# Single PSUM banks for the feed-forward's inner units, and an empty step between a norm's variance and the use of its root

## The chip, the cores and the metric

The kernel is one program on one core of a Trainium2 chip. It runs two transformer blocks over a batch of 2 sequences of 2048 tokens, 128 channels wide, in float32. The metric is the time on the device in microseconds; the median of several runs is given. The engines are named as in the profile: PE is TensorE (matrix products and transposes), PEld its weight loads, ACT is ScalarE, DVE is VectorE, POOL is GpSimd, SP is SyncE (it issues most DMA transfers). PSUM is the memory that PE writes to, SBUF the one that the other operands lie in.

## The reference, cut to what matters

Each of the two blocks is an attention layer and then a stack of local-attention layers with feed-forward; both are modulated by a conditioning vector. The first block has a chunked attention with a memory and then 6 local layers (16 heads, window 32); the second has a causal linear attention with its own norms and a feed-forward, and then 2 local layers (8 heads, window 64). A local layer is, cut short:

```python
h = shift(x)                        # half of the channels come from the token before
q, k, v = split(h @ Wqkv)           # q and k: l2norm, scale, rotary tables
x = x + local_attention(q, k, v) @ Wo
...
mu = h.mean(-1); var = ((h - mu) ** 2).mean(-1)
xn = (h - mu) / sqrt(var + 1e-5) * g + b
a, gate = split(xn @ W1 + b1)       # 341 inner units each
x = x + (a * gelu(gate)) @ W2 + b2
```

The linear attention between the two stacks has three norms of the same form: one ahead of q, k and v, one ahead of its feed-forward, and one that makes the input of the second stack.

## The kernel before, in words

The profile's first 640 us or so are the first block's attention (`l0_attention`), which the change does not touch. Everything else is in `local_models`. It treats 8 local layers (6 of the first model, 2 of the second) as one long list of tiles: 32 tiles of 128 tokens per layer (16 places in the sequence for each of the 2 sequences, the sequences alternating). Channels or head columns lie on the partitions in the layer's state, tokens on the partitions during attention.

A single loop over the tiles (L1505 and on) works on several of them at once. In turn i it writes down:

- the scores of tile i+1 (`ps_s`), their exponential on ACT (`weights_exp`, L1008) and their norm;
- the projection of q and k of tile i+3 (`project`: `ps_qk` L871, the square `sq` on ACT L873, rotary products `r` and `t` on DVE, sums on POOL). A tile of the first model has two projections, one of the second model has one;
- **place A** for a feed-forward step, between the first and the second projection;
- the transposes of tile i's weights (`ps_pT` L1026, copied by ACT, L1027), the values of tile i+2 (`ps_v` L951, copied by ACT, L952), the weighted sum of tile i (`ps_o` L1043), the transposes of q and k of tile i+2 (`ps_turn` L923), the transposes of the sum (`ps_oT` L1059, copied by ACT L1060);
- **place B** for a feed-forward step;
- the output projection of tile i (`ps_y` L1071).

After four tiles of one sequence a feed-forward over their 512 tokens is appended to the list `steps` as six small functions: `centre` (one matmul that subtracts the mean, and a square on ACT, L1098), `variance` (four matmuls to `ps_var` L1107, plus epsilon on DVE `fve` L1112, power -1/2 on POOL `frt` L1114), `scale` (four transposes that spread the root, `ps_r` L1120, product on DVE `fx` L1123), `gate` (three matmuls `ps_f` L1141, of 128, 128 and 85 units, and three Gelus on ACT L1151), `up` (the other three `ps_f`, and a product with the Gelus on DVE L1158) and `down` (`ps_fy` L1166, and the sum into the state on DVE, L1172). `step()` runs the first of the list. So a tile takes up to two steps; two feed-forwards fall due in every eight tiles, which have sixteen places.

The linear attention is cut in the same way into 27 steps per block of 512 tokens (`linear`, L1236), some of them an empty `rest`. Its list, `lsteps`, has six places a tile and is filled after the last layer of the first model; its eight blocks run among the last tiles of that model and the first of the second. A tile of the second model's first layer that needs a block not yet finished runs `lstep` until it is (the loop on `ready`). The steps of its norms use the same `centre`, `variance` and `scaled`.

PSUM has two pools: `psA` with two slots of two banks (`wide`: `ps_qk`, `ps_s`, two of the three parts of `ps_f`, and three tiles of the linear attention), and `psT` with four slots of one bank (`bank`: everything else named above, and the third part of `ps_f`). A slot is taken in turn when its earlier tile has been read.

The order in which the instructions stand on each engine is not that of the code alone: a list scheduler sets it when the program is built, with the order of the code as priority and its own estimates of duration. It can bring an instruction forward past others on its engine.

Of the kernel before, what the change touches and what calls it, by code (L numbers as in the profile page):

```python
# [24 lines left out]
HSZ = (128, 128, 85)  # L25
# [47 lines left out]
def tile_kernel(ctx: ExitStack, tc: tile.TileContext, a: dict, out: bass.AP):  # L73
# [27 lines left out]
    def bc(ap, shape):  # L101
        return ap.to_broadcast(list(shape))
# [605 lines left out]
    def local_models(mA, mB, hs0):  # L708
# [3 lines left out]
        wk = ctx2.enter_context(tc.tile_pool(name="f_k", bufs=1))  # L712
        lw = ctx2.enter_context(tc.tile_pool(name="l_w", bufs=1))
# [3 lines left out]
        def wide(name):  # L717

            return psA.tile([128, 1024], F32, tag="A", name=f"ps_{name}")

        def bank(name):
            return psT.tile([128, 512], F32, tag="T", name=f"ps_{name}")
# [362 lines left out]
        def step():  # L1085
            if steps:
                steps.pop(0)()

        def lstep():
            if lsteps:  # L1090
                lsteps.pop(0)()


        def centre(S, x, pool, keep):
            p = bank("c")
            nc.tensor.matmul(p, lhsT=cen, rhs=x, start=True, stop=True)  # L1096
            S["sq"] = pool.tile([128, 512], F32, name="fsq")
            nc.scalar.activation(S["sq"], p, AF.Square)  # L1098
            if keep:
                S["xc"] = pool.tile([128, 512], F32, tag="t1", name="xc")  # L1100
                nc.scalar.copy(S["xc"], p)

        def variance(S, pool):
            p = bank("var")
            sq = S.pop("sq")
            for j in range(4):
                nc.tensor.matmul(  # L1107
                    p[:, j:j + 1], lhsT=sq[:, j * 128:(j + 1) * 128], rhs=onesm[:, 0:1],
                    start=True, stop=True,
                )  # L1110
            ve = pool.tile([128, 4], F32, name="fve")
            nc.vector.tensor_scalar(ve, p[:, 0:4], 1e-5, None, ALU.add)  # L1112
            S["rt"] = pool.tile([128, 4], F32, name="frt")
            nc.gpsimd.tensor_tensor(S["rt"], ve, bc(nhalf, (128, 4)), ALU.pow)  # L1114

        def scaled(S, x, out):
            p = bank("r")
            rt = S.pop("rt")
            for j in range(4):
                nc.tensor.transpose(  # L1120
                    p[:, j * 128:(j + 1) * 128], bc(rt[:, j:j + 1], (128, 128)), ident
                )
            nc.vector.tensor_tensor(out, x, p, ALU.mult)  # L1123


        def feed_forward(g, b, blk):
            m, l = layers[g]
            n0 = blk * 512
            x = hs[1][:, b, n0:n0 + 512]
            S = {}  # L1130

            def scale():
                S["x"] = wk.tile([128, 512], F32, tag="fsq", name="fx")
                scaled(S, x, S["x"])

            def hidden(base):
                pw = wide("f")
                ps_ = [pw[:, 0:512], pw[:, 512:1024], bank("f")]
                for c, sz in enumerate(HSZ):
                    o = base + 128 * c  # L1140
                    nc.tensor.matmul(  # L1141
                        ps_[c][0:sz], lhsT=wts[g, "w1"][:, o:o + sz], rhs=S["x"],
                        start=True, stop=True,
                    )
                return ps_

            def gate():
                for c, p in enumerate(hidden(HID)):
                    sz = HSZ[c]
                    u = S[c] = wk.tile([128, 512], F32, name=f"u{c}")  # L1150
                    nc.scalar.activation(  # L1151
                        u[0:sz], p[0:sz], AF.Gelu, bias=wts[g, "c"][0:sz, 3 + c:4 + c]
                    )

            def up():
                for c, p in enumerate(hidden(0)):
                    sz = HSZ[c]
                    nc.vector.scalar_tensor_tensor(  # L1158
                        S[c][0:sz], p[0:sz], wts[g, "c"][0:sz, c:c + 1], S[c][0:sz],
                        ALU.add, ALU.mult,  # L1160
                    )

            def down():
                p = bank("fy")
                for c, sz in enumerate(HSZ):
                    nc.tensor.matmul(  # L1166
                        p, lhsT=wts[g, "w2"][0:sz, c, :], rhs=S[c][0:sz],
                        start=(c == 0), stop=(c == 2),
                    )
                for lo, sh in ((0, 0), (64, 1)):  # L1170
                    cs = slice(n0 + sh, n0 + sh + 512)
                    nc.vector.scalar_tensor_tensor(  # L1172
                        hs[0][lo:lo + 64, b, cs], p[lo:lo + 64, :], m.vec[lo:lo + 64, l, 8:9],
                        hs[1][lo:lo + 64, b, cs], ALU.add, ALU.add,
                    )
                if l == m.depth - 1:
                    lsteps.extend((linear if m is models[0] else output)(b, blk))

            steps.extend((
                lambda: centre(S, x, wk, False), lambda: variance(S, wk), scale, gate, up, down,  # L1180
            ))

        def outer(b, k, gate, x):
# [55 lines left out]
        def linear(b, k):  # L1239
            S = {}  # L1240
# [8 lines left out]
            def a0():  # L1249
                outer(b, k, mA, S["x"])  # L1250

            def rest():
                pass

            def a3():
                xc = S.pop("xc")
# [140 lines left out]
            def f3():  # L1397
# [9 lines left out]
                ready.add((b, k))  # L1407

            return (
                fetch, rest, a0, lambda: centre(S, S["x"], lw, True), lambda: variance(S, lw), a3,  # L1410
                rest, lambda: centre(S, S["h"], lw, False), b2, b3, b4, rest, c1, c2, c3, c4, d1,
                rest, lambda: centre(S, S["x1"], lw, False), lambda: variance(S, lw), d4, e1, e2,
                rest, lambda: centre(S, S.pop("x"), lw, True), lambda: variance(S, lw), f3,
            )


# [37 lines left out]
        for i in range(-3, n):  # L1454
            j = i + 3
            lstep()
            if 0 <= i + 1 < n:
                scores(i + 1)
# [3 lines left out]
            if j < n:  # L1462
                g, b, t = tiles[j]
                jj = j % per
                nu = len(layers[g][0].units)
                more = g < last
                if g == second and t % 4 == 0:
                    while (b, t // 4) not in ready:
                        lstep()
                project(j, 0)  # L1470
                if more and jj == 4:
                    load_proj(g + 1, 0)
                if more and jj == 6 and g + 1 == second:
                    models[1].consts()
                if jj == 6 and g == second - 1:
                    linear_consts()
                if more and jj == 8:
                    factors(g + 1)
                    if 2 == 2:
                        load_out(g + 1)  # L1480
                if more and jj == 18:
                    load_ff(g + 1)
                if more and jj == 22:
                    fold_ff(g + 1)
                if more and jj == per - 1:
                    load_proj(g + 1, 1)
                lstep()
# [23 lines left out]
            if i >= 0:  # L1511
                g, b, t = tiles[i]
                project_out(i)
                if 2 == 1 and i % per == per - 1 and g < last:
                    load_out(g + 1)
                if t % 4 == 3:
                    feed_forward(g, b, t // 4)
# [9 lines left out]
    with ExitStack() as ctx2:  # L1527
        local_models(m0, m1, hs0)
# [63 lines left out]
```

## Time and profile before

| what | value |
|---|---|
| median of 3 runs | 5047.73 us (5043.81 to 5053.04) |
| the profiled execution's own time | 5053.27 us |
| its span | 5051.4 us |
| mean granted clock of PE | 0.959 |
| instructions | 171478 |
| `ps_f` matmuls (L1141) | 768, 600 ns each, 365.5 us busy |
| Gelu of the feed-forward, 128 partitions (L1151) | 128, 683 ns each |
| table loads of ACT at L1151, L1008, L1381 | 62, 68 and 7 of 1283 ns |
| root on POOL (`frt` L1114) | 96, 1026 ns each |
| `ps_r` transposes (L1120) | 352, 286 ns each; 23.5 us idle before them |

In the tables of waits, a line names the engine, the tile and line of the instruction that waited, what released it, and then the microseconds in total, the number of waits and the longest. In the timeline, a line is start, duration, engine, line, operation, the tile written and the tiles read, and a count where several alike are put together; in square brackets is the idle time ahead of it. A table load (`ACT_TABLE_LOAD`) is what ACT does when the next function is not among those loaded: here between Exp and Gelu.

### The profile page before, as it was taken

The page shows a single profiled execution, that of the slowest core. Times are in us where ns is not written, and L with a number is a line of the kernel's source. Part 1 is how long each engine was busy: PE and PEld are TensorE (multiplying, and loading weights), DVE is VectorE, ACT ScalarE, POOL GpSimd, SP SyncE. Part 2 cuts the span into 40 slices and gives each one's busy share as a digit, 9 for nine tenths or more (in the row PEclk, how much of TensorE's full clock was granted, in tenths as well). Part 3 has the DMA queues.
Part 4 walks back from the last instruction along what each step waited for, and adds up shares of the span by engine and source line. Part 5 has one row for each costly group of instructions (what it writes and reads, how often), then busy time and mean ns, then how long its engine had stood idle before and what let it go on. Part 6 is the DMA issues. An engine that isn't in the chain of part 4 may idle for free.

```text
span 5051.4 us, 171478 instructions
## 1 busy us (share of the span) xinstructions
PE 4682.5 (93%) x75042; PEld 3190.3 (63%) x75042; DVE 3883.5 (77%) x6760; ACT 2796.3 (55%) x4645; POOL 2761.1 (55%) x1650
## 2 busy tenths in 40 slices
PE   5667799999999999999999999999999998999998
PEld 4445566666666666666666666666666665566565
DVE  6993488788887887788887788787767766688886
ACT  3323356666666665566665566566555654555554
POOL 3331366666665666566666666665544533355553
PEclk8777799999999999999999999999999999999999
DMA  2000222222222322232222322232222211111111
GB/s 76 1 1 24 83 69 66 63 71 74 70 63 63 82 70 63 62 81 72 63 64 65 81 67 64 64 82 64 52 53 54 54 44 36 41 46 48 53 54 40
DMA packets 222491, 295.63 MB, mean 59 GB/s; under 512 B 75657, under 2 KB 95409, under 8 KB 221745
## 3 DMA queue, kind: packets, MB, share of 16 engines
q1 hardware_dynamic: 221744, 284.67, 21.8%
q8 instruction: 592, 9.70, 0.8%
q14 instruction: 155, 1.26, 0.1%
HBM read 40.98 MB, written 10.75 MB: 10 GB/s over the span
## 4 chain that ended last, share of the span: by engine, by line
PE 75%; DVE 6%; ACT 4%; issue 2%; POOL 2%; DMA 0%; SPq 0%; ACTq 0%; POOLq 0%; DVEq 0%
PE ps_qk L871 15%; PE ps_y L1071 8%; PE ps_turn L923 8%; PE ps_o L1043 7%; PE ps_s L991 7%; PE ps_v L951 6%; PE ps_f L1141 6%; PE ps_oT L1059 4%; PE ps_pT L1026 4%; PE ps_fy L1166 3%; PE ps_var L1107 1%; PE ps_c L1096 1%; PE ps_s L982 1%; POOL r L892 1%; ACT sq L873 1%
## 5 line engine op out<-in xcount | busy, mean ns | idle before, releaser
L892 POOL TENSOR_TENSOR r<-r,t 128x1024 f32<-128x1024 f32 x448 | 1059.9, 2366 | 1162.4 <-DVE t L886 1075.2
L873 ACT ACTIVATE sq<-ps_qk 128x1024 f32<-128x1024 f32 x448 | 459.1, 1025 | 1369.4 <-PE ps_qk L871 1353.2
L904 POOL TENSOR_TENSOR r<-r,rq_y 128x1024 f32<-128x1024 f32 x448 | 845.5, 1905 | 268.0 <-DVE rq_y L180 267.1
L871 PE MATMUL ps_qk<-wp,hs 128*128 128x512 f32 x1792 | 883.6, 616 | 30.1 <-DVE rq_y L180 15.4
L886 DVE TENSOR_TENSOR t<-ps_qk,tb 128x1024 f32<-128x1024 f32 (+1 forms) x512 | 552.8, 1080 | 180.5 <-POOL r L892 180.4
L1017 POOL TENSOR_TENSOR sm<-sm,rs 128x1024 f32<-128x1024 f32 x256 | 488.0, 1906 | 293.6 <-DVE rs L1016 196.2
L881 DVE TENSOR_TENSOR r<-ps_qk,tb 128x1024 f32<-128x1024 f32 (+1 forms) x512 | 547.7, 1070 | 103.1 <-ACT sq L873 102.1
L897 DVE TENSOR_REDUCE ps_qk<-sq 128x16 f32<-128x1024 f32 x448 | 549.6, 1227 | 13.5
L871 PEld LDWEIGHTS ps_qk<-wp,hs 128*128 128x128 f32 x1792 | 311.6, 191 | 351.5 <-issue 260.2
L1071 PEld LDWEIGHTS ps_y<-oT,wo 128*128 128x128 f32 x3584 | 440.8, 193 | 122.4 <-issue 71.1
L1071 PE MATMUL ps_y<-oT,wo 128*128 128x128 f32 x3584 | 482.8, 282 | 18.7 <-ACT oT L1060 18.2
L923 PE MATMUL ps_turn<-ident,r 128*128 128x128 f32 x3584 | 470.6, 281 | 22.9 <-issue 12.0
L1043 PEld LDWEIGHTS ps_o<-v,pT 64*32 64x32 f32 (+1 forms) x26624 | 343.6, 108 | 226.9 <-ACT pT L1027 114.9
L951 PE MATMUL ps_v<-wp,hs 128*128 128x512 f32 x896 | 446.9, 598 | 5.9 <-ACT o L1436 3.7
L999 DVE TENSOR_REDUCE mx<-ps_s 128x16 f32<-128x1024 f32 (+1 forms) x256 | 312.9, 1222 | 166.4 <-PE ps_s L991 162.1
L1043 PE MATMUL ps_o<-v,pT 64*32 64x64 f32 (+1 forms) x26624 | 392.5, 222 | 41.0 <-ACT pT L1027 23.3
L923 PEld LDWEIGHTS ps_turn<-ident,r 128*128 128x128 f32 x3584 | 395.2, 143 | 54.4 <-issue 15.8
L991 PE MATMUL ps_s<-kT,qT 64*32 64x64 f32 (+1 forms) x26624 | 400.5, 230 | 3.9 <-ACT kT L928 3.2
L1049 ACT COPY on<-ps_o 128x512 f32<-128x512 f32 x448 | 244.4, 589 | 244.1 <-PE ps_o L1043 244.1
L991 PEld LDWEIGHTS ps_s<-kT,qT 64*32 64x32 f32 (+1 forms) x26624 | 330.1, 107 | 70.3 <-issue 37.3
L1141 PE MATMUL ps_f<-fx,w 128*128 128x512 f32 (+1 forms) x768 | 365.5, 600 | 2.6 <-DVE fx L1123 1.7
L1026 PEld LDWEIGHTS ps_pT<-ident,sm 128*128 128x128 f32 x2048 | 245.7, 142 | 149.6 <-issue 142.1
(266 smaller groups left out, 7693.6 us busy)
## 6 DMA issues: line engine op xcount, KB each, us to landing
v<-vn SPq DMA_DIRECT2D x1276, 128.0 KB
v<-vn SPq DMA_DIRECT2D x744, 64.0 KB
v<-vn SPq DMA_DIRECT2D x64, 256.0 KB
wp<-in_L_ffn_Wqkv SPq DMA_DIRECT2D x20, 512.0 KB
xD<-xb SPq DMA_DIRECT2D x24, 256.0 KB
xb<-xD SPq DMA_DIRECT2D x24, 256.0 KB
cs<-in_cos SPq DMA_DIRECT2D x128, 32.0 KB
cs<-in_sin SPq DMA_DIRECT2D x128, 32.0 KB
```

Source lines behind the costliest of these rows:

```text
L871: nc.tensor.matmul(pq[:, js], lhsT=hw, rhs=wts[g, u][:, js], start=True, stop=True)
L881: nc.vector.tensor_tensor(r[:, es].rearrange("p (h d) -> p h d", d=DH), pq[:, es].rearrange("p (h d) -> p h d", d=DH), bc(tb[:, 0, s].unsq ...
L886: nc.vector.tensor_tensor(t2[:, es].rearrange("p (h s d) -> p h s d", s=2, d=32), pq[:, es].rearrange("p (h s d) -> p h s d", s=2, d=32)[: ...
L892: nc.gpsimd.tensor_tensor(r, r, t2, ALU.add)
L897: nc.vector.tensor_reduce(pq[:, 16 * v:16 * v + 16], st[i].pop(("sq", v)).rearrange("p (h d) -> p h d", d=DH), AX.X, ALU.add,)
L904: nc.gpsimd.tensor_tensor(rv, rv, bc(y[:, 16 * v:16 * v + 16].unsqueeze(2), (128, 16, DH)), ALU.mult)
L923: nc.tensor.transpose(p[:, c * 128:(c + 1) * 128], r[:, cs], ident)
L951: nc.tensor.matmul(p, lhsT=hw, rhs=wv, start=True, stop=True)
L991: nc.tensor.matmul(sp[W * w:W * w + W, c0:c0 + 2 * W], lhsT=qT[64 * q:64 * q + 64, cc, W * w:W * w + W], rhs=kT[64 * q:64 * q + 64, cc, W ...
L1043: nc.tensor.matmul(po[s][W * w:W * w + W, co:co + 64], lhsT=pT[kp, q, c, W * w:W * w + W], rhs=v2[kp, w, co:co + 64], start=True, stop=True,)
L1071: nc.tensor.matmul(py[:, 0:128], lhsT=wts[g, "o"][:, c * NO + s, :], rhs=oT[:, s, c, :], start=(c + s == 0), stop=(c == 3 and s == NO - 1),)
L1141: nc.tensor.matmul(ps_[c][0:sz], lhsT=wts[g, "w1"][:, o:o + sz], rhs=S["x"], start=True, stop=True,)
```

## The change

Three edits, all in `local_models`:

1. `hidden`, which both `gate` and `up` call, takes three single banks for its three parts instead of one wide slot and a bank. The feed-forward no longer uses `psA`.
2. `rest`, an empty function, stands outside `linear` so that both lists can use it, and the feed-forward's list has it between `variance` and `scale`: seven steps instead of six.
3. The linear attention's list has it in three places more, between `variance` and the step that uses the root (`a3`, `d4`, `f3`): 30 steps instead of 27. The norm in `b2` and `b3` is as it was.

No instruction is added, removed or altered by it, apart from what the scheduler reorders and from the table loads that follow from ACT's order.

```diff
+        def rest():
+            pass
+
         def lstep():
...
             def hidden(base):
-                pw = wide("f")
-                ps_ = [pw[:, 0:512], pw[:, 512:1024], bank("f")]
+                ps_ = [bank("f") for _ in HSZ]
                 for c, sz in enumerate(HSZ):
...
             steps.extend((
-                lambda: centre(S, x, wk, False), lambda: variance(S, wk), scale, gate, up, down,
+                lambda: centre(S, x, wk, False), lambda: variance(S, wk), rest, scale, gate, up,
+                down,
             ))
...
-            def rest():
-                pass
...
             return (
-                fetch, rest, a0, lambda: centre(S, S["x"], lw, True), lambda: variance(S, lw), a3,
+                fetch, rest, a0, lambda: centre(S, S["x"], lw, True), lambda: variance(S, lw), rest,
+                a3,
                 rest, lambda: centre(S, S["h"], lw, False), b2, b3, b4, rest, c1, c2, c3, c4, d1,
-                rest, lambda: centre(S, S["x1"], lw, False), lambda: variance(S, lw), d4, e1, e2,
-                rest, lambda: centre(S, S.pop("x"), lw, True), lambda: variance(S, lw), f3,
+                rest, lambda: centre(S, S["x1"], lw, False), lambda: variance(S, lw), rest,
+                d4, e1, e2,
+                rest, lambda: centre(S, S.pop("x"), lw, True), lambda: variance(S, lw), rest,
+                f3,
             )
```

## The prediction

> **What bounds the kernel now.** I read the page first (busy shares, slices, chain), then busy time by stage, TensorE's waits by stage, then the timeline of single tiles.
>
> ```profile
> span 5051.4 us, 171478 instructions
> ...
> PE 4682.5 (93%) x75042; PEld 3190.3 (63%) x75042; DVE 3883.5 (77%) x6760; ACT 2796.3 (55%) x4645; POOL 2761.1 (55%) x1650
> ...
> PE 75%; DVE 6%; ACT 4%; issue 2%; POOL 2%; DMA 0%; SPq 0%; ACTq 0%; POOLq 0%; DVEq 0%
> ```
>
> TensorE is busy 93% of the span and makes 75% of the chain; no other engine makes more than 6%. Cut by stage (us, then busy us and counts of PE, PEld, DVE, ACT, POOL, clock, DMA share, GB/s):
>
> ```profile
> 0.00:820.00 820.00, 615.46 (x8421) 433.14 (x8422) 575.60 (x994) 316.05 (x607) 320.24 (x199) 0.82 0.16 44
> 820.00:4080.00 3260.00, 3177.12 (x58858) 2186.42 (x58857) 2588.08 (x4250) 1961.45 (x3213) 1993.21 (x1164) 0.99 0.26 67
> 4080.00:5051.00 971.00, 889.96 (x7765) 570.78 (x7764) 719.82 (x1517) 518.83 (x827) 447.64 (x288) 0.97 0.16 44
> ```
>
> Between 820 and 4080 us TensorE is idle for 82.9 us of 3260, after that for 81 us of 971. A change that alters no matmul can win only from these 164 us. What they wait for, in the two windows:
>
> ```profile
> PE ps_o L1043 <- issue: 17.4, 10, 2.6
> PE ps_y L1071 <- ACT oT L1060: 14.4, 38, 0.7
> PE ps_turn L923 <- issue: 12.0, 12, 2.4
> PE ps_qk L871 <- DVE rq_y L180: 11.2, 5, 2.7
> PE ps_r L1120 <- POOL frt L1114: 8.7, 6, 2.3
> ```
> ```profile
> PE ps_o L1043 <- ACT pT L1027: 21.3, 33, 2.8
> PE ps_r L1120 <- POOL frt L1114: 14.7, 8, 3.6
> ```
>
> (us, times, longest.) The wait that the empty places address, frt before ps_r, sums to 23.5 us in 14 cases. Each lies at 3605 us or later, most of them up to 4400 us, where the linear attention's norms run among the tiles; in the six steady layers of the first model there is none. A wide PSUM slot held by the feed-forward shows nowhere as such a wait. The last view is the tile whose first feed-forward place holds `up`, in the third layer:
>
> ```profile
> 2023.21 1.28 ACT L1151 ACT_TABLE_LOAD   x1
> ...
> 2027.70 1.98 PE L871 MATMUL ps_qk<-wp,hs 128*128 128x512 f32 x4
> ...
> 2029.72 1.02 ACT L873 ACTIVATE sq<-ps_qk 128x1024 f32<-128x1024 f32 x1 [3.38 <-PE ps_qk L871]
> ...
> 2030.77 1.28 ACT L1008 ACT_TABLE_LOAD   x1
> ...
> 2036.56 1.57 PE L1043 MATMUL ps_o<-v,pT 64*32 64x64 f32 x128
> ```
>
> ScalarE was idle for 3.38 us ahead of sq, so a Gelu and its table load late in a tile are paid from slack. Between the projections and ps_o it has little: sq, exp, sq, two pT copies must all be done before ps_o.
>
> **What the Trainium skill says.** "ScalarE: Activation LUTs", Table sets: the hidden batching unit, puts exp and gelu in different sets and says to batch by set; What ACT_TABLE_LOAD costs prices a switch at some 2.7 us with its drain. The trace agrees that they switch: 138 loads at 1.283 us each; I use 1.28. "PSUM — Partial Sum Buffer", Specifications, has 8 banks of 2 KiB per partition, and its rule on one matmul's output limits that to a bank. So the kernel's two wide slots and four single ones are all there is: what the feed-forward frees in one pool it takes from the other. No page bears on the scheduling of the steps.
>
> **The change part by part.** Times are from T0, the end of a tile's first ps_qk; durations are those of the steady tiles in before's timeline and its groups (three Gelus 1.83, a pair of pT copies 1.07, exp 1.05), and the order on each engine is that of the changed program as built.
>
> 1. The empty places issue no instruction and no DMA, but move all later steps. There are two feed-forward places a tile, A between the two projections and B ahead of ps_y, and two feed-forwards per eight tiles. Before, six steps each: A holds centre, scale, up; B holds variance, gate, down. With seven, the first one's gate and the second one's variance, scale and up fall in A, the first one's up and the second's centre and gate in B. One gate in two now stands in A.
>
> 2. Norms of the steady layers: TensorE's work between ps_var and ps_r grows from 5.0 to 13.6 us, but no wait stood there. Gain 0. The rq_y waits (five of about 2.3 us, one per layer, behind POOL's tables) keep their cause; 0.
>
> 3. Gate in A, first model (six layers of four such tiles: 24). ScalarE's order becomes sq, exp, load, three Gelus, sq, two pT copies: 1.03+1.05+1.28+1.83+1.02+1.07 = 7.28 us, from T0+0.05, so 7.33. TensorE comes to ps_o after ps_f 2.58, the second ps_qk 1.75, ps_pT 0.87 and ps_v 1.72: 6.92. Stall 0.4 us (0.2 to 0.5). Queued behind on ScalarE are the pT copies, then the vn copies; ps_o waits for both.
>
> 4. Up in A, first model (24 instead of 48, which showed no stall). The three ps_f now take three of the four single banks, so ps_v's first bank is that of the first pT and waits for its copy: the second sq ends at 5.5, the copy at 6.1, TensorE is there at 5.56. Stall 0.5 (0.3 to 0.6). VectorE, which releases ps_f, has sum order mx 1.22, sm 1.22, u 0.74, r 1.22, t 1.21, rs 1.21, u: the second ps_f bank is free only at about 6.05, the same time. What hid all this before is that two of the three ps_f stood in a wide slot.
>
> 5. Place B covers oT's copy for ps_y. Shortfall with nothing there 1.06, with variance 0.6, with a full step 0.07; summed over eight tiles 3.6 before, 3.5 to 3.75 after. 0. So the first model loses 24 x (0.4+0.5) = 21.6; I take 20, as some stalls let ScalarE catch up and shorten a later wait (0 to 40).
>
> 6. Second model (two layers, one projection a tile). With gate in A, ScalarE's program order splits in about six of eight such tiles: load, one Gelu, load, exp, sq, load, two Gelus, two copies. The program's table loads go from 138 to 152. From the end of ps_s: exp done 4.0, ps_qk 4.75, sq 5.95, load 7.25, Gelus 8.5, pT copies 9.6, where TensorE would be at ps_o at 6.65. Stall 3.0, less one up in A (0.5) and an rq_y wait (0.4) that go: 2.3 a case, six cases, 14 us (4 to 25).
>
> 7. Linear attention's norms (3590 to 4400 us). Cover between ps_var and ps_r rises: most had 1.3 to 3.4 us and now 3 to 5; fve and frt with their queues need about 5. The sum of shortfalls goes from 52 to 30, so 23.5 x 30/52 = 13.5 stays: -10 us. With three places more (30 steps instead of 27), each block's linear attention ends half a tile later, its xb load and the store of x with it; the loop that waits for a block may start issuing sooner. Unknown, from -20 to +10. The tail adds 0 to 2 us.
>
> Sum: 20+14-10 = +24. The profiled execution took 5053.27 us (span 5051.4 and 1.9 around it), and would take 5077; it lies 5.5 above the median of the runs, so the median would go from 5047.7 to 5072.
>
> **The rivals.**
>
> Faster (other side). Mechanism: ps_v and ps_o take the longer way, but TensorE's weight loads and its 0.2 to 0.3 us of issue put it at ps_o just after ScalarE, so steps 3 and 4 cost nothing; the frt waits vanish. For it: items 3 and 4 are margins of 0.4 us on sums of 7. Against: the before kernel's tile above has ps_o 6.88 us after T0, which is my sum. Price: the whole 23.5, so 5024; with half of it 5036. It decides if the stalls are under 0.2 us each.
>
> No change. Step 7 gains its full 20, the steady layers lose 10 (0.4 for each of 24 pairs of a gate and an up) and the second model 10: about 5048. For it: the shares are alike in size. Against: ps_o already waits for pT, 21.3 us in 33 cases, in the window where ScalarE is loaded most.
>
> Much slower. The late ps_v moves vn, and the single banks run short in every tile that has a gate or up, B too; ends of the ranges 40+25+10: +75, 5123. For it: four single banks must carry f, pT, v, turn, o, oT and y. Against: steps in B are followed by ps_y, whose bank comes free early.
>
> That the empty place does not do what it says: in the steady layers there is nothing to cover, as said, so there it only shifts steps.
>
> **How the numbers follow.** Forecast 5072: 0.56. Faster 0.24, no change 0.14, much slower 0.06. Measured noise allows telling 0.2%, 10 us, from no change. Own range of the forecast 5058 to 5092; the range for 8 in 10 reaches into the faster case and half into the worst: 5028 to 5098. Faster by over 0.2%: 0.24; within 0.2%: 0.16; slower: 0.60, from the same cases (0.02 of the forecast's low end falls within 0.2%).
>
> **What would show it.** Step 3: ps_o waits for pT up to 3590 us, about 24 of 0.4 us. Step 4: ps_v waits for pT or u there, about 24 of 0.5. Step 6: 152 table loads, and one ps_o or ps_v wait of about 3 us per eight tiles of the second model. Step 7: the frt wait falls from 23.5 to about 13. Wrong: no ps_o or ps_v waits in the steady layers, or PE's idle time between 820 and 3590 us not larger than before.

## The result, and the profile after

The changed kernel takes 5077.59 us (median of 6, 5074.73 to 5086.36) against 5045.77 us (median of 6 runs of the kernel before): a ratio of 1.0067, 95% interval 1.0051 to 1.0084, so slower by 0.5 to 0.8%. The forecast was 5072. The profiled execution has a span of 5073.7 us, 22.3 more than before. Between the medians the difference is 31.8 us: the profiled execution of before took 5053.27 us, 7.5 above the median of its runs here, that of after 5075.82, 1.8 below. So the profiles account for 22 of some 32 us.

Busy time by stage of the kernel after, in the columns of the prediction's second block:

```profile
0.00:820.00 820.00, 604.50 (x8388) 430.26 (x8419) 575.34 (x993) 315.66 (x607) 320.78 (x199) 0.82 0.16 44
820.00:4080.00 3260.00, 3175.54 (x58719) 2177.63 (x58720) 2570.83 (x4228) 1952.95 (x3201) 1991.20 (x1162) 1.00 0.26 66
4080.00:5074.00 994.00, 906.24 (x7927) 578.35 (x7916) 737.05 (x1540) 548.72 (x852) 449.23 (x290) 0.98 0.16 43
```

In the middle stage TensorE is as busy as before, 3175.5 against 3177.1 us of 3260, but it got through 58719 matmuls instead of 58858. A wait between two matmuls whose ends are modelled can hide in "busy"; the count of matmuls done in the same time is then the better sign.

TensorE's waits in the kernel after, first from 820 to 4080 us, then to the end:

```profile
PE ps_y L1071 <- ACT oT L1060: 18.8, 55, 0.5
PE ps_v L951 <- ACT pT L1027: 12.0, 27, 0.7
PE ps_qk L871 <- DVE rq_y L180: 10.7, 5, 2.7
PE ps_o L1043 <- issue: 9.1, 11, 2.0
PE ps_turn L923 <- issue: 9.0, 12, 1.3
```
```profile
PE ps_v L951 <- ACT u L1153: 13.1, 6, 2.3
PE ps_o L1043 <- ACT pT L1027: 12.7, 22, 1.4
PE ps_out L1436 <- DVE xb L1190: 10.3, 4, 4.6
PE ps_r L1123 <- POOL frt L1117: 4.6, 4, 1.5
```

The wait for the root, 23.5 us before, is down to 4.9 in the whole kernel: the empty step does what it was put there for. In its place stand waits of ps_v, for the pT copy in the first model and for the Gelu in the second, neither of which was among the long ones before. The waits put down to "issue" fell from 29.4 to 18.1 us in the same window.

To see where the 22.3 us come from I cut both executions at the same pieces of work, not at the same times: at the first projection ps_qk, at the 337th (168 tiles of the first model done, 21 of its 24 periods of eight tiles), at the 421st (the linear attention done), at the last one, and at the end. "Period" below is always eight tiles. Durations of before, and what each kernel adds to them, in us:

| kernel | to the first ps_qk | first model, 336 ps_qk | linear stage, 84 ps_qk | second model, 27 ps_qk | tail | span |
|---|---|---|---|---|---|---|
| before | 582.1 | 2923.3 | 1131.8 | 339.2 | 75.0 | 5051.4 |
| after | -1.3 | +11.6 | -6.0 | +12.8 | +5.3 | +22.3 |
| e1_banks | -11.7 | -10.0 | -7.9 | -0.1 | +0.6 | -29.1 |
| e2_ffrest | +0.8 | +21.7 | +5.6 | +8.9 | +10.6 | +47.5 |
| e3_linrest | -7.7 | +3.3 | +47.3 | -0.1 | +3.9 | +46.7 |
| e4_even | -6.1 | -23.2 | +60.4 | -0.7 | +7.2 | +37.6 |
| e5_lin3 | -3.4 | +5.8 | +1.9 | -0.4 | +1.8 | +5.7 |
| e6_even3 | -6.8 | -21.3 | +4.7 | -0.8 | +6.6 | -17.5 |
| e7_after3 | -5.7 | +18.4 | +48.2 | +12.7 | +5.3 | +78.9 |
| e8_queues | -5.1 | -46.5 | +1.0 | +4.5 | +14.6 | -31.6 |
| e9_nolin | -0.8 | +13.6 | +15.9 | +9.7 | +5.2 | +43.6 |
| e10_queues_wide | -1.6 | -53.1 | -28.6 | +2.2 | +12.5 | -68.6 |
| e11_second_even | -13.1 | +15.3 | +4.1 | -0.9 | +5.4 | +10.7 |
| e12_queues_lin | -9.4 | -51.7 | -14.0 | -1.2 | +13.8 | -62.5 |

These are single executions. How far they can be trusted shows in the first column, which no kernel changes and which moves by 13 us (the granted clock there was 0.76 in before and 0.81 in e11), and in the first model: e3 and e5, whose feed-forward and tiles are those of before, have +3.3 and +5.8, and after, e7, e9 and e11, which share theirs, from +11.6 to +18.4. So up to 7 us in the second column are nothing; the second model's part repeats better (within 1 us of before in e1, e3, e4, e5, e6 and e11, which all have its gates in B). The linear stage also holds the last 3 periods of the first model and about half of the second model's 8.

The waits of TensorE explain only a part of these columns. Below is the linear stage, cut at the same projections (start and end, length, busy us and count of PE, its clock, DMA share, GB/s), in before, e3 and e10:

```profile
3505.40:4637.20 1131.80, 1062.38 (x13144) 0.97 0.18 48
3500.90:4680.00 1179.10, 1083.08 (x13151) 0.95 0.17 46
3450.70:4553.90 1103.20, 1043.68 (x13154) 0.98 0.19 50
```

Of e3's 47.3 us, 26.6 are idle time and 20.7 longer busy time for the same work; of e10's gain of 28.6, 9.9 are idle and 18.7 busy. The granted clock moves with it (0.967, 0.951 and 0.985 in three digits). In before, 73 `ps_y` matmuls that lie in stretches of half the clock take 421 ns in the median, the others 275. In the stage e3 has 41 us more at half the clock than before, e10 41 us less; from these numbers I estimate that the clock makes some 14 us of either's change in busy time. It is not the whole: after has e10's clock in this stage and only 4.8 us less busy time than before. Whether the waits bring the clock down or only go with it, no run here separates.

### The profile page after: what moved, and what is told of

Read it like the earlier page. It is cut to its first block, busy times and chain, and to the rows that moved or that the text cites. A ratio compares the mean times of both kernels' runs of the same rounds, so it can differ in the third digit from the quotient of the medians.

```text
span 5073.7 us, 171261 instructions
## 1 busy us (share of the span) xinstructions
PE 4686.3 (92%) x75012; PEld 3186.2 (63%) x75042; DVE 3883.2 (77%) x6760; ACT 2817.3 (56%) x4659; POOL 2761.2 (54%) x1650
## 3 DMA queue, kind: packets, MB, share of 16 engines
q1 hardware_dynamic: 221744, 284.67, 21.7%
## 4 chain that ended last, share of the span: by engine, by line
PE 74%; DVE 6%; ACT 5%; issue 3%; POOL 2%; DMA 0%; SPq 0%; ACTq 0%; POOLq 0%; DVEq 0%
PE ps_qk L871 15%; PE ps_y L1071 8%; PE ps_turn L923 8%; PE ps_v L951 7%; PE ps_o L1043 7%; PE ps_s L991 6%; PE ps_f L1143 6%; PE ps_oT L1059 4%; PE ps_pT L1026 3%; PE ps_fy L1168 3%; PE ps_c L1099 1%; PE ps_var L1110 1%; PE ps_s L982 1%; ACT sq L873 1%; POOL r L892 1%
## 5 line engine op out<-in xcount | busy, mean ns | idle before, releaser
L897 DVE TENSOR_REDUCE ps_qk<-sq 128x16 f32<-128x1024 f32 x448 | 549.7, 1227 | 13.8
L923 PE MATMUL ps_turn<-ident,r 128*128 128x128 f32 x3584 | 465.7, 280 | 20.8 <-issue 10.7
L951 PE MATMUL ps_v<-wp,hs 128*128 128x512 f32 x896 | 445.7, 604 | 31.2 <-ACT u L1153 14.8
L923 PEld LDWEIGHTS ps_turn<-ident,r 128*128 128x128 f32 x3584 | 391.7, 142 | 52.9 <-issue 13.5
L1043 PE MATMUL ps_o<-v,pT 64*32 64x64 f32 (+1 forms) x26624 | 397.6, 222 | 23.5 <-ACT pT L1027 13.8
L1143 PE MATMUL ps_f<-fx,w 128*128 128x512 f32 (+1 forms) x768 | 353.5, 596 | 5.2 <-ACT g L1382 3.1
L1015 DVE TENSOR_REDUCE rs<-sm 128x16 f32<-128x1024 f32 (+1 forms) x256 | 309.9, 1211 | 24.1 <-ACT sm L1008 23.2
```

The lines of the kernel that those rows point to most:

```text
L897: nc.vector.tensor_reduce(pq[:, 16 * v:16 * v + 16], st[i].pop(("sq", v)).rearrange("p (h d) -> p h d", d=DH), AX.X, ALU.add,)
L923: nc.tensor.transpose(p[:, c * 128:(c + 1) * 128], r[:, cs], ident)
L951: nc.tensor.matmul(p, lhsT=hw, rhs=wv, start=True, stop=True)
L1043: nc.tensor.matmul(po[s][W * w:W * w + W, co:co + 64], lhsT=pT[kp, q, c, W * w:W * w + W], rhs=v2[kp, w, co:co + 64], start=True, stop=True,)
L1143: nc.tensor.matmul(ps_[c][0:sz], lhsT=wts[g, "w1"][:, o:o + sz], rhs=S["x"], start=True, stop=True,)
```

## The experiments

Twelve kernels, each timed beside the kernel before; ratios are with their 95% interval.

**The three edits one at a time.** First the banks alone.

```diff
-                pw = wide("f")
-                ps_ = [pw[:, 0:512], pw[:, 512:1024], bank("f")]
+                ps_ = [bank("f") for _ in HSZ]
```

> Only the three single banks, six steps as before: every gate stays in place B and every up in place A, two in each period of eight tiles; the built program keeps 138 table loads. If the single banks cost where an up stands in A (the trace of after shows ps_v waiting for the pT copy there, about 0.5 us a case), there are twice as many cases as in after, 48 in the first model: 24 us, and some 5 us more at the end of the kernel, where ps_out waits longer: about +20 to +30 us, near 5070. Rival, it is the places of the steps alone that cost: 0 to +5 us, near 5048.

Measured: 5030.97 us, ratio 0.9979 (0.9967 to 0.9991). Faster, against both theories. TensorE's waits of e1 from 820 to 3590 us:

```profile
PE ps_v L951 <- ACT pT L1027: 15.8, 40, 0.4
PE ps_y L1071 <- ACT oT L1060: 13.4, 36, 0.4
PE ps_qk L871 <- DVE rq_y L180: 10.9, 5, 2.7
PE ps_turn L923 <- issue: 4.8, 9, 1.6
```

The wait that I expected of the banks is there: 40 cases of 0.4 us, two in each of 20 periods. It is half of what an up in A costs with single banks: in such a tile of the first model ps_o starts 7.80 us after T0 in the median (e1, e4 and after), with the wide slot 6.88 (before) or 6.87 (e2). But something larger went. In the same window the kernel before has

```profile
PE ps_o L1043 <- issue: 16.5, 9, 2.6
...
PE ps_turn L923 <- issue: 12.0, 12, 2.4
```

that is 28.5 us, of which e1 keeps 5.0 (4.8 and 0.2 at ps_o). One of these waits in the kernel before, in the timeline of TensorE and the view of the DMA queues between 2370 and 2374 us:

```profile
2369.95 1.54 PE L1043 MATMUL ps_o<-v,pT 64*32 64x64 f32 x124
...
2373.44 0.30 PE L1043 MATMUL ps_o<-v,pT 64*32 64x64 f32 x4 [1.95 <-issue]
```
```profile
DMA  0000000000600000000000000000000000000000
...
q8 instruction: 1, 0.02, 1.5%
```

TensorE stops after 124 of the 128 small matmuls of ps_o, for 1.95 us, with all its data there. The only transfer in these 4 us is one 16 KB packet of the instruction queue, a little after 2371 us. In the trace's records all 25 gaps of over 0.3 us at ps_o, ps_turn and ps_s in this window (31.9 us; five of them, 3.6 us, stand in the table as waits for ACT or POOL) end 2.2 to 2.8 us after such a packet began, 2.4 in the median. Waits for data are not tied to the packets so: the 35 waits of over 0.3 us of ps_o for the pT copy in e8_queues, below, end anywhere from 0.2 to 7.7 us after one. TensorE waits for its own instructions. e3, whose tiles here are those of before, has 36.6 us of such gaps, e2 19.9, after 14.4, e1 7.1 and e4 7.1. The wide slot with an up in place A has the most of them, the single banks with six or eight steps the least. That ps_v's new waits give the supply of instructions time to catch up would fit, but e10_queues_wide, below, has few of these gaps without such waits. Why they go stays open.

Then the feed-forward's empty step alone, with the wide slot:

```diff
-                lambda: centre(S, x, wk, False), lambda: variance(S, wk), scale, gate, up, down,
+                lambda: centre(S, x, wk, False), lambda: variance(S, wk), rest, scale,
+                gate, up, down,
```

> Only the empty step in the feed-forward, the wide slot kept: half of the gates go to place A, and B holds scale, centre and an empty step in turn; the built program has 154 table loads. If the places cost (B covers the oT copy less, about 1.2 us per period of eight tiles by a comparison of the two traces, 24 periods; a gate in A 0.2; in the second model about 4 us per period, 8 periods, from split table loads): +50 us, near 5095. Rival, the single banks alone cost: 0 us, 5046, and no ps_v wait of 3 us in the second model.

Measured: 5101.02 us, ratio 1.0114 (1.0099 to 1.0130): the places cost, about what was expected. The first model loses 21.7, the second 8.9 in its last part, the tail 10.6. In the first model's stage the loss of after is the sum of e1's gain and e2's loss (-10.0+21.7 = 11.7; measured 11.6); so close a fit is chance, as the same first model gave up to 18.4 in another run.

Then the linear attention's three empty steps alone:

```diff
-                fetch, rest, a0, lambda: centre(S, S["x"], lw, True), lambda: variance(S, lw), a3,
+                fetch, rest, a0, lambda: centre(S, S["x"], lw, True), lambda: variance(S, lw), rest,
+                a3,
...
+                rest, lambda: centre(S, S["x1"], lw, False), lambda: variance(S, lw), rest,
+                d4, e1, e2,
+                rest, lambda: centre(S, S.pop("x"), lw, True), lambda: variance(S, lw), rest,
+                f3,
```

> Only the three empty steps in the linear attention: the steady layers are the same program as before. By my prediction the frt waits fall from 23.5 to 13.5 us and the time by 10 us, to 5036. By the trace of after (frt waits about 5 us in all, and the tiles of the second model's start 27 us ahead of before) it is 25 to 30 us, near 5018. Rival, the later end of the linear attention gives it back: 5046.

Measured: 5103.39 us, ratio 1.0118 (1.0102 to 1.0134). All three expectations miss: a loss of near 60 us, where the same steps stand beside a slight gain of the stage in after. The waits of TensorE from 3590 to 4400 us, first in before, then in e3:

```profile
PE ps_r L1120 <- POOL frt L1114: 21.6, 11, 3.6
PE ps_aT L1355 <- DVE at L1347: 6.5, 3, 3.0
```
```profile
PE ps_aT L1355 <- DVE ps_qk L167: 19.0, 4, 4.7
PE ps_var L1107 <- ACT fsq L1098: 9.2, 7, 2.8
PE ps_num L1335 <- DVE sum L1326: 9.1, 3, 3.5
PE ps_r L1120 <- POOL frt L1114: 4.9, 5, 1.9
```

The wait for frt is down to 4.9 us in this window (10.2 in the whole kernel), as the empty steps mean it to be, and three others take its place. They belong to the 26.6 us of idle time that were added to the stage; the other 20.7 us of its loss are busy time, as said above. The longest kind, in e3's timeline (lines of DVE, and the one of PE that waits):

```profile
3769.73 1.23 DVE L897 TENSOR_REDUCE ps_qk<-sq 128x16 f32<-128x1024 f32 x1
...
3772.19 1.21 DVE L897 TENSOR_REDUCE ps_qk<-sq 128x16 f32<-128x1024 f32 x1
3773.32 0.67 DVE L1347 TENSOR_TENSOR at<-ps_num,rd 128x512 f32<-128x512 f32 x1
3773.92 0.18 DVE L167 TENSOR_SCALAR ps_qk<-ps_qk 128x32 f32<-128x32 f32 x1
3774.14 1.09 PE L1355 MATMUL ps_aT<-ident,at 128*128 128x128 f32 x4 [4.75 <-DVE ps_qk L167]
```

ps_aT transposes `at`, which DVE writes (L1347) only after the two 1.2 us sums of the tile's q and k and a copy between them. The table names L167, which ended just before ps_aT was let go; by the tiles that it reads, what it waited for is the line above, `at`. Step c3 has been given to the tile just when DVE is taken up by the q and k norms, and c4 follows at the next place.

All three edits together are 34 us slower (0.67% of 5046), singly, by their ratios, 11 faster, 57 slower and 60 slower, 106 in sum. Some 70 us less than the sum is an interaction. In the table, where the spans add to 65 us against 22.3, most of it stands in one column: the linear stage's three single values add to 45 us, and in after it is -6.

**The first attempt at a repair.** Against the changed kernel. If the odd number of steps makes most of the loss, a second empty step in the feed-forward (eight steps, two feed-forwards filling sixteen places) puts gates back into B and ups into A:

```diff
-                lambda: centre(S, x, wk, False), lambda: variance(S, wk), rest, scale, gate, up,
-                down,
+                lambda: centre(S, x, wk, False), lambda: variance(S, wk), rest, rest, scale,
+                gate, up, down,
```

> The changed kernel with a second empty step in the feed-forward (eight steps): gates are back in B, ups back in A, the single banks and the linear attention's empty steps stay; the built program has 140 table loads. If the odd number of steps makes most of the loss: the second model gets back some 30 us and place B its cover, the ups in A cost 0.5 us in 48 cases instead of 24: about 5035 to 5045. If the single banks make the loss: 5077 or more.

Measured: 5078.61 us, ratio 1.0073 (1.0061 to 1.0086), which looks like the second expectation. By stages it is not: the first model is 23.2 us ahead of before and 35 ahead of after, the second model's +12.8 is gone (-0.7), and the linear stage is 60 us behind before, 66 behind after. One number hid large ones of opposite sign. The first model is also 13 us ahead of e1's, which has the same places for up and gate; the five waits of ps_qk for rq_y, 10.9 us in e1, are not in e4's table, so the second empty step removes a wait that nothing here was meant to touch.

**Why the linear stage turns.** A linear step has six places a tile. With 30 steps, a multiple of six, each kind of step falls in the same place in every block; with 27 it alternates. In after the first feed-forward has its down in A, in e3 and e4 in B, so the whole list begins three places apart. Three runs move nothing else: three empty steps ahead of the very first block.

```diff
-            return (
+            lead = (rest,) * (3 if b + k == 0 else 0)
+            return lead + (
```

> e3_linrest with three empty steps more, ahead of the first block of the linear attention only: each of its later steps stands three places (half a tile) later, as in the changed kernel, where the first feed-forward's down is in place A. Theory: with 30 steps and six places a tile each kind of step always falls in the same place of the tile, so that what e3_linrest lost is the place, not the number of steps: ps_aT's waits (19 us in e3) go, the loss of 50 us between 3590 and 4590 us becomes a gain of 20 to 30: near 5020. Rival: three empty steps per block delay the linear attention itself and hold up the second model's tiles: 5100 or more.

> e4_even with the same three empty steps ahead of the first linear block. By the theory of the place: the first model's layers as in e4 (24 us ahead of before), the linear stage gains 20 to 30 us on before instead of losing 50, the second model as before: near 5000. Rival, the number of steps: near 5078, as e4.

> The changed kernel with the same three empty steps ahead of the first linear block, which puts its steps in the places that they have in e3_linrest. By the theory of the place: the linear stage loses what it gained in after (some 34 us) and up to 50 more: 5110 to 5150. Rival: near 5078, as after.

Measured: e5 5054.24 us, ratio 1.0018 (1.0009 to 1.0027); e6 5035.83, 0.9977 (0.9969 to 0.9986); e7 5128.11, 1.0160 (1.0139 to 1.0181). The linear stage goes from +47.3 to +1.9 (e3 to e5), from +60.4 to +4.7 (e4 to e6) and from -6.0 to +48.2 (after to e7). Three steps that do nothing are worth some 50 us either way; the place decides (with the order that the scheduler makes of it, which changes too), and the rival, their number, is out. Of this swing 21 to 24 us are TensorE's idle time in each pair and 23 to 33 its busy time for the same work, with a granted clock of 0.95, 0.94 and 0.95 in the bad place and 0.97, 0.97 and 0.98 in the good one. But half of the expectation failed: in the better place the stage gains nothing on before, where 20 to 30 us were expected. e5's waits of TensorE from 3590 to 4400 us say why:

```profile
PE ps_o L1043 <- ACT pT L1027: 12.0, 7, 3.3
PE ps_qk L1296 <- DVE z L1287: 5.3, 4, 1.9
PE ps_c L1099 <- ACT h L1259: 5.2, 2, 2.6
PE ps_num L1335 <- DVE rq_y L180: 4.7, 1, 4.7
```

frt is down to 3.9 us in the whole kernel, and these stand in its place (ps_o's wait for pT was 4.9 us in the same window of before, the others 1.7 us or not in its table): the stage's idle time is 73.2 us, in before 69.4.

**What the linear steps are worth inside the change.** The changed kernel with `linear`'s list as it was before:

> The changed kernel without the three empty steps in the linear attention (27 steps), the other two edits kept: what these steps are worth inside the change. By my prediction they gain 10 us: 5088. By the stages of the runs so far (the linear stage -8 us with the banks alone, +6 with the feed-forward's empty step alone, -6 in after) about 4 us: near 5082. Rival, they cost in the change as they do alone in e3_linrest (57 us): near 5020.

Measured: 5093.29 us, ratio 1.0095 (1.0077 to 1.0113), 0.28% above after's ratio, some 14 us; the two intervals overlap, so the size is uncertain. frt holds ps_r up for 19.3 us again. In the table the linear stage is 21.9 us longer than in after, 15.3 of them idle time. So inside the change the three steps gain, some 14 to 22 us; outside it they cost 60.

**The second model.** Its timeline in after, in a tile whose gate stands in A (lines of ACT, and the one of PE that waits):

```profile
4738.20 1.28 ACT L1153 ACT_TABLE_LOAD   x1
...
4740.90 0.69 ACT L1153 ACTIVATE u<-ps_f,c 128x512 f32<-128x512 f32 x1 [1.42 <-PE ps_f L1143]
4742.92 1.28 ACT L1008 ACT_TABLE_LOAD   x1 [1.33 <-DVE rq_y L180]
...
4746.20 1.28 ACT L1153 ACT_TABLE_LOAD   x1
4747.50 1.26 ACT L1153 ACTIVATE u<-ps_f,c 128x512 f32<-128x512 f32 x2
4748.23 1.13 PE L951 MATMUL ps_v<-wp,hs 128*128 128x512 f32 x2 [2.31 <-ACT u L1153]
```

The three Gelus are split by an Exp, with a table load on each side, and ps_v waits 2.31 us for a bank that the later Gelus hold. A load costs its 1.28 us and no more here: the Gelu at 4747.50 begins 0.02 us after it. The split is not all. In the part where the second model runs alone, ps_v waits 9.3 us for u, but ps_out also waits 5.7 us for `xb` (three times, not once in before), as the steps that write the result out have moved too, and ps_o waits 5.3 us less for pT. To price both, the second empty step goes into the second model's feed-forwards only:

```diff
-                lambda: centre(S, x, wk, False), lambda: variance(S, wk), rest, scale, gate, up,
-                down,
+                lambda: centre(S, x, wk, False), lambda: variance(S, wk),
+                *(rest,) * (1 if m is models[0] else 2), scale,
+                gate, up, down,
```

> The changed kernel with a second empty step in the feed-forward of the second model's two layers only, so that their gates stand in place B; the built program has 140 table loads instead of 152. By the stages of after, a period of eight tiles of the second model goes from 102 or 104 us to 98: eight periods, 25 to 30 us: near 5050. By my prediction's 14 us: 5064. Rival, the table loads are not what costs there: 5077.

Measured: 5068.68 us, ratio 1.0050 (1.0032 to 1.0069). Where the second model runs alone, the 12.8 us of after are gone to -0.9, with the loads and with both waits, which this run does not tell apart. But the linear stage, which holds the other half of its periods, is 10 us slower than in after, so the total gains 9 us by the ratios, and the two intervals overlap: less than was expected by the stages, and not clearly different from either 5064 or the rival's 5077. What of those 10 us belongs to the linear steps and what to the tiles was not separated.

**A version with fixed places.** Two lists, so that centre, variance and scale run in A only and gate, up and down in B only, where they cover the wait of ps_y for oT. The empty steps in these lists only keep the two in step with each other. First with single banks:

```diff
-                lambda: centre(S, x, wk, False), lambda: variance(S, wk), scale, gate, up, down,
+                *(rest,) * b, lambda: centre(S, x, wk, False), lambda: variance(S, wk), scale,
             ))
+            steps_b.extend((rest,) * (1 if b or steps_b else 2) + (gate, up, down))
...
                 turn_out(i)
-            step()
+            step_b()
```

> Neither empty step of the change; single banks as in e1_banks, and the feed-forward's steps in two lists: centre, variance and scale run in place A only, gate, up and down in place B only, where they cover ps_y's wait for oT. By the phases of before, place B's shortfall goes from 3.6 to 2.3 us per period of eight tiles (24 periods: 30 us) and ps_v's waits for the pT copy (15.8 us in e1) go, as no ps_f stands in A: 35 to 45 us less than e1's 5031 in all but the linear stage, whose steps start elsewhere (from -30 to +50): near 4995 with an even linear stage. Rival, the cover of ps_y is worth nothing, since TensorE's supply of instructions decides: near 5031.

> e8_queues with the wide slot in place of the single banks: no ps_f stands in A, where the wide slot was followed by the waits for instructions (28.7 us at ps_o and ps_turn up to 3590 us in before, 6 in e1, some 8 in e8). If the wide slot gains or loses only through what it does in A, this is as fast as e8: near 5018, with less than 10 us of these waits. Rival, the wide slot itself costs wherever it stands: 5030 or more, with 20 us or more of them.

Measured: e8 5018.02 us, ratio 0.9945 (0.9928 to 0.9961); e10, the same with the wide slot, 4978.36 us, 0.9865 (0.9844 to 0.9886). Both beat the kernel before, and neither fits its expectation: e8 lies between its 4995 and 5031, e10 40 us under its 5018. The first model gains 46.5 and 53.1 us. e10's waits of TensorE from 820 to 3590 us:

```profile
PE ps_y L1071 <- ACT oT L1060: 14.1, 37, 0.4
PE ps_s L982 <- DVE rq_y L180: 8.8, 5, 2.1
PE ps_turn L923 <- issue: 5.2, 8, 1.3
```

The table of waits does not show the expected cause: ps_y's wait, which B was to cover, is 14.1 us and was 13.4. The busy time does. These are the ps_y matmuls of the first model, cut at the same projections, in before and in e10 (columns as in the linear stage above):

```profile
582.10:3505.40 2923.30, 352.20 (x2640) 0.99 0.28 70
580.50:3450.70 2870.20, 339.07 (x2640) 0.99 0.28 71
```

The same 2640 matmuls take 13.1 us less, and as much in e8: about half of the 26 us that 30 us in 24 periods make for these 21. The waits for instructions are down too, from 28.5 us at ps_o and ps_turn to 5.4 in e10 and 5.5 in e8. So e1's gain is not a virtue of single banks: few of these waits are left with the wide slot too if no ps_f stands in A. In all, e10's gain in the first model is 25.2 us of idle time and 27.9 of busy time, e8's 8.3 and 38.2; the busy time beyond ps_y's was not traced to a cause. e10 being 40 us faster than e8 was not foreseen. In e8 ps_o waits for pT 18.1 us in the first model, in e10 it is not among the waits; and the linear stage is 30 us ahead of e8's, for which I have no tested reason. Two thirds of what it gains on before are busy time, as said above.

Last, the linear steps in the best version:

```diff
-                fetch, rest, a0, lambda: centre(S, S["x"], lw, True), lambda: variance(S, lw), a3,
+                fetch, rest, a0, lambda: centre(S, S["x"], lw, True), lambda: variance(S, lw), rest,
+                a3,
...
```

(and the other two, and the three ahead of the first block)

> e10_queues_wide with the linear attention's three empty steps and, so that its steps stand as in e5_lin3, three more ahead of its first block. frt still holds ps_r up for 30 us in e10. If these steps are worth what they are worth inside the change (16 us by e9_nolin): near 4962. If the waits only move to other steps, as in e5_lin3 (+8 us): 4978 to 4990.

Measured: 4994.37 us, ratio 0.9889 (0.9869 to 0.9910), 16 us above e10, just beyond the second expectation. frt's wait fell from 32.7 us to 18.5 in the whole kernel, and TensorE's idle time in the linear stage by 3.0 us; but its busy time there rose by 17.6, with a clock of 0.97 against 0.98, and the stage is 15 us worse. Cutting that wait down doesn't pay here.

## Why the prediction was right, and where it wasn't

The direction and the range held; the forecast was +24 us, the medians differ by 32. By its own steps:

1. The places (part 1) are as it said, and e2 shows that they cost: the feed-forward's empty step alone takes 57 us.
2. The steady layers' norms (part 2) gave nothing, and the rq_y waits stayed (11.2 and 10.7 us in the middle window): right.
3. Gate in A, first model (part 3): a ps_o wait of 0.4 us in 24 cases was forecast, and there is no such wait in the table up to 3590 us. In a tile like that ps_o starts 6.8 us after T0 (6.92 forecast) on the first pT copy and runs 1.81 us in the median instead of 1.57, as the second copy comes late: 0.24 us, hidden in the busy time. The term was half as large as taken.
4. Up in A, first model (part 4): 24 waits of 0.5 us at ps_v for pT were forecast, 12 us; 25 were measured up to 3590 us, 11.5 us. Right as a wait, and with more cases in e1. As a cost it was too small: ps_o of such a tile comes 0.9 us later, not 0.5. And it was wrong as a price of the banks: alone they also remove 23.5 us of waits for instructions (e1, 28.5 to 5.0), and in after such waits fell by 11.3 (29.4 to 18.1), which the prediction had listed in its table ("issue") and taken as fixed.
5. Place B (part 5) was set at 0, from a shortfall of 3.6 us a period before and 3.5 to 3.75 after. ps_y's wait went from 13.4 to 18.8 us in the first model's window, and the same 2640 ps_y matmuls took 358.1 us instead of 352.2. Together that is 11.3 us, 0.5 a period. By the median distances from ps_oT to the next ps_qk, a centre in B covers only a part of the oT copy and a scale next to nothing. This term was put at nothing and was not.
6. Second model (part 6): 14 us forecast from split table loads. Its own sum is slightly off: 3.0 less 0.5 and 0.4 is 2.1 a case, not 2.3, so 13. The loads are there (152 in the trace, 138 before), and ps_v waits for u in 8 cases, 14.8 us in the whole kernel: right in kind and size. What it left out is the wait of ps_out for `xb`, 5.7 us where the second model runs alone. There the loss is 12.8 us in 3.4 of 8 periods, and e11 takes all of it away. Prorated over eight periods that would be 30; this is an estimate, as the first half runs among the linear steps.
7. The linear norms (part 7): -10 forecast, from frt falling to 13.5 us. frt fell to 4.9, and the three steps are worth some 14 to 22 us inside the change (e9). The reason given, more cover for frt, is only the half of it: the same steps cost 60 us in e3, where frt fell to 10.2. Which other waits the new places meet decides, and how long TensorE is busy with the same work. The allowance of -20 to +10 was about wide enough for the place that after has, and far too narrow for a place three steps on (e7, 50 us worse); that after lies at the good end is an accident of its seven steps.
8. The tail (0 to 2 forecast): 5.3 us. TensorE's idle time in it is no longer than before (18.6 us, before 19.2), and the wait of ps_out for `xb` there is 4.6 us in both. It does more: 36 ps_f matmuls are left for it instead of 28, as the last feed-forward comes later.

The prediction named as a sign of being wrong that TensorE's idle time between 820 and 3590 us is not larger than before. This sign came. In that window, before and after:

```profile
820.00:3590.00 2770.00, 2711.83 (x51775) 1867.85 (x51775) 2237.28 (x3646) 1690.07 (x2778) 1755.86 (x1022) 1.00 0.27 69
820.00:3590.00 2770.00, 2711.82 (x51464) 1862.84 (x51463) 2230.33 (x3628) 1680.46 (x2763) 1746.19 (x1018) 1.00 0.27 69
```

TensorE is idle for 58.2 us in both; after got through 311 matmuls fewer. The new waits at ps_v and ps_y, 16.9 us, are made up for by the waits for instructions and a few others that went, and the loss of the first model (11.6 us, 10.5 of them busy time at the same work) lies where the prediction did not look. Its bound, that a change which alters no matmul can win only from TensorE's 164 idle us, falls with it: e8 won 38 us of busy time in the first model alone.

So the number was near partly by luck: terms that were too small (an up in A, B, the second model, the tail) stood against gains that were not foreseen (the waits for instructions, and more from the linear steps than 10). The faster rival, frt's waits gone and the rest hidden, had its first half come true. The rival that the empty step doesn't do what it says fell: frt's wait went down wherever the linear steps were put in, to between 3.9 and 10.2 us, in e12 only from 32.7 to 18.5.

## What to carry to other kernels

In a pipeline where small steps are dealt out to fixed places, an empty step is not free: it moves every later one to another place, and what counts is what each step then meets on the other engines. Count steps against places per period: if the one is a multiple of the other, every block meets the same neighbour, good or bad, and a shift by half a tile is a test that costs one line. When parts of a change are tried alone, cut the executions at the same work, since a total within 0.1% of another can hide 35 us gained and 66 lost. And compare the busy time of the same work as well as the waits: here about half of the large differences stood in busy time, where no table of waits shows them.

## What the runs showed of the hardware that was not expected

TensorE can outrun its instructions. A group of 128 small matmuls with their 128 weight loads takes 1.5 us, and 25 times in 2770 us of the kernel before, within such groups or at the transposes behind them, TensorE then stood for 0.3 to 2.6 us until 2.4 us (median) after a 16 KB packet of the instruction queue had begun; a packet itself takes about 1 us (median 1.04). The same matmuls in another order have 31.9 us of these gaps in before, 14.4 in after, 7.1 in e1 and 7.1 in e4. Nothing in the kernel's text waits there, and the table of waits calls most of it "issue" (28.3 of the 31.9 us).

A load of ACT's tables takes 1.283 us, and little is lost around it: in before, 130 of the 137 loads that stand between two other ACT instructions have less than 0.1 us of idle time on either side.
